# Graph attention in two layers: the attention's output turned by VectorE and by way of DRAM, scores and sums in column halves

## The chip, the cores and the metric

The kernel runs on one core of one Trainium2 chip. The metric is device time in microseconds for one execution. Before the change the median of three runs is 2571.63 us (2571.38 to 2572.58).

## What is computed

Two graph layers work on `x` of 16 graphs, 1024 nodes and 256 channels, all in float32. The first layer holds the attention that the change touches; the second (an aggregation over the graph, two matrix products with batch norms) runs beside it and after it. Cut to what matters:

```python
# --- layer 0 ---
h = jnp.maximum(_layernorm(x, axis=-1), 0.0)
...
g = jnp.einsum('bcn,bnm->bcm', fea, Wg)            # fea is h turned, Wg the weighted graph
g = jax.nn.relu(g * para.reshape(1, C, N))
q = jnp.transpose(g, (0, 2, 1)).reshape(B, N, h, hd).transpose(0, 2, 1, 3)
kv = (x @ kv_w).reshape(B, N, 2, h, hd).transpose(2, 0, 3, 1, 4)
k, v = (kv[0], kv[1])
attn = jax.nn.softmax(jnp.einsum('bhnd,bhmd->bhnm', q, k) * scale, axis=-1)
out = jnp.einsum('bhnm,bhmd->bhnd', attn, v)
return out.transpose(0, 2, 1, 3).reshape(B, N, C)
# x = x + that; then layer 1 on the result
```

There are four heads of 64 channels. The kernel takes the exponential without subtracting a maximum; a flag at the end would call a second, shifted version of the program if the sums had left a safe range.

## The kernel before

A *unit* is one graph `b`, one pair of heads `k` (128 channels) and one half `f` of the nodes that ask (512 of 1024): 64 units. A unit has four *steps*, each for 256 of the nodes that are asked about, so there are 256 steps, 16 to a graph.

`attention` (line 1032) writes the order out by hand, and the engines follow program order. In step `s` it issues:

1. `scores` (line 906): for two blocks of 128 asked nodes and the two heads, the products of keys and queries into PSUM (`sc`, two buffers[...]), then ScalarE's exponential into `p` (four buffers).
2. what is entered under `at_top` for this step: `sums` (line 977) and `finish` (line 1004) of the unit before.
3. what is entered under `adds`: `add_output` (line 1015) of the unit before.
4. VectorE's additions of the new `p` into `acc` (lines 941 and 944), from which the softmax's sums come.
5. `values` (line 946): the products of the step before's `p` with the values, into `o` (one PSUM buffer). After a unit's last step ScalarE copies `o` to `os` (line 964, two buffers).
6. work of the *background*, as much as a planner's costs say is due: queries, keys and values of the next graph, and layer 1's aggregation of the graph before. Its products go through the helper `product` (line 168), which splits each into two column halves: 128 contracted rows by 64 output rows, on each half of the array.
7. what is entered under `at_end`: `fold` (line 966), which turns and reduces `acc`.

If a unit's last values product falls in step `s`, its folds come at the end of steps `s` and `s+1`, `sums` in `s+3`, `finish` and `add_output` in `s+4`. The last unit of all has a shorter order. `finish` makes four TensorE transposes of 128x128 from `os` into PSUM (`ot`), and `add_output` multiplies them by the reciprocals of the sums (line 1018) and adds to `x` (line 1024).

The scores use the array in row halves: the two heads' 64 channels lie on partitions 0 to 63 and 64 to 127, and each product has 64 contracted rows and 128 output rows. The values and all background products use column halves. `sums` and `finish` use the whole array.

Loads run on SyncE's queue in program order (`adj`, `para`, `aht`, `ht`, `x`), stores of `y` (line 769), of `x` (line 785) and of `hsq_d` (line 412) on GpSimd's. `squares` and `gathered` (lines 402 and 414) already turn the layer's input by VectorE in squares of 32 and regroup it by way of DRAM.

Of the kernel before, what the change touches and what calls it, by code (L numbers as in the profile page):

```python
# [10 lines left out]
F32 = mybir.dt.float32  # L11
AF = mybir.ActivationFunctionType
ALU = mybir.AluOpType
AX = mybir.AxisListType
# [3 lines left out]
P = 128  # L18
# [5 lines left out]
def gnn_two_layers_kernel(  # L24
# [12 lines left out]
    nc = tc.nc  # L37
    B, N, C = x.shape
    H1 = w1_t.shape[1]
    NT = N // P  # L40
    CC = C // P
    HC = H1 // P
    HD = C // HEADS
    FB = 512
    NH = N // FB
    TH = 2
    NP = NT // TH
    HW = P // 2
# [3 lines left out]
    const = ctx.enter_context(tc.tile_pool(name="const", bufs=1))  # L52
# [17 lines left out]
    y1_d = [dram.tile([P, HC, FB], F32, name=f"y1_d{i}") for i in range(B * NH)]  # L70

    hsq_d = [dram.tile([P, CC, N], F32, name=f"hsq_d{b}") for b in range(B)]
    csum_d = [dram.tile([N], F32, name=f"csum_d{b}") for b in range(B)]
    dinv_d = dram.tile([N], F32, name="dinv_d")

    UNITS = B * CC * NH
# [3 lines left out]

    SQ = 32
    NS = P // SQ
    same = const.tile([P, NS, SQ], F32, name="same")
    nc.vector.tensor_reduce(
        same[:, 0, :], ident.rearrange("p (a r) -> p r a", r=SQ), AX.X, ALU.add
    )
    for i in range(1, NS):
        nc.vector.tensor_copy(same[:, i, :], same[:, 0, :])
    group = const.tile([P, NS], F32, name="group")
    nc.vector.tensor_reduce(group, ident.rearrange("p (a r) -> p a r", r=SQ), AX.X, ALU.add)  # L90

# [5 lines left out]
    def layers(shifted):  # L97
# [808 lines left out]
        def scores(b, k, f, g):  # L906


            made = []
            for m in (2 * g, 2 * g + 1):  # L910
                sc = ps_sc.tile([P, 2, FB], F32, tag="sc", name=f"sc_{b}_{k}_{f}_{m}")
                for e in range(2):
                    r = slice(e * HD, (e + 1) * HD)
                    nc.tensor.matmul(  # L914
                        sc[:, e, :],
                        ks[b][k][r, m * P : (m + 1) * P],
                        qs[b][k][r, f * FB : (f + 1) * FB],
                        start=True,
                        stop=True,
                    )  # L920
                pr = p4.tile([P, 2, FB], F32, tag="p", name=f"p_{b}_{k}_{f}_{m}")
                nc.scalar.activation(pr, sc, AF.Exp)  # L922
                made.append(pr)
            return made

        class Unit:
# [19 lines left out]
            def values(self, g, prs):  # L946

                b, k, f = self.at
                if g == 0:
                    self.o = ps_o.tile([P, FB], F32, tag="o", name=f"o_{self.name}")  # L950
                for i, pr in enumerate(prs):
                    m = 2 * g + i
                    for e in range(2):
                        r = slice(e * HD, (e + 1) * HD)
                        nc.tensor.matmul(  # L955
                            self.o[r, :],
                            vs[b][k][:, m, r],
                            pr[:, e, :],
                            start=(m == 0),
                            stop=(m == NT - 1),  # L960
                        )
                if g == NG - 1:
                    self.os = p2.tile([P, FB], F32, tag="os", name=f"os_{self.name}")
                    nc.scalar.copy(self.os, self.o)

            def fold(self, e):

# [9 lines left out]
            def sums(self):  # L977

                b, k, f = self.at
                J = FB // P  # L980
                if k == f == 0:
                    invs[b] = p2.tile([P, CC, NH, J, 2], F32, tag="inv", name=f"inv_{b}")
                self.inv = invs[b][:, k, f]
                pt = ps_t.tile([P, FB], F32, tag="t", name=f"sums_{self.name}")[:, : 2 * J * NS]
                nc.tensor.matmul(
                    pt,
                    same.rearrange("p a r -> p (a r)"),
                    self.part.rearrange("p e c -> p (e c)"),
                    start=True,
                    stop=True,  # L990
                )
                tmp = p1.tile([P, 2 * J, NS + 1], F32, tag="group", name=f"group_{self.name}")
                nc.vector.tensor_mul(
                    tmp[:, :, :NS],
                    pt.rearrange("p (c a) -> p c a", a=NS),
                    group.unsqueeze(1).to_broadcast([P, 2 * J, NS]),
                )
                nc.vector.tensor_reduce(tmp[:, :, NS], tmp[:, :, :NS], AX.X, ALU.add)
                nc.vector.reciprocal(
                    self.inv.rearrange("p j e -> p e j"),  # L1000
                    tmp[:, :, NS].rearrange("p (e j) -> p e j", e=2),
                )

            def finish(self):
# [9 lines left out]

            def add_output(self):
                b, k, f = self.at
                J, pt = FB // P, self.out
                nc.vector.tensor_mul(
                    self.os.rearrange("p (j e c) -> p j e c", j=J, e=2),
                    pt.rearrange("p (j e c) -> p j e c", j=J, e=2),  # L1020
                    self.inv.unsqueeze(3).to_broadcast([P, J, 2, HD]),
                )
                dst = xs[b][:, f * J : (f + 1) * J, k * P : (k + 1) * P]
                nc.vector.tensor_add(dst, self.os.rearrange("p (j c) -> p j c", c=P), dst)
                if k == CC - 1 and f == NH - 1:
                    inv = invs[b].rearrange("p k f j e -> p (k f j e)")
                    nc.vector.tensor_reduce(seen[:, 0, b : b + 1], inv, AX.X, ALU.max)
                    nc.vector.tensor_reduce(seen[:, 1, b : b + 1], inv, AX.X, ALU.min)
                if k == CC - 1:
                    complete.add((b, f))  # L1030

        def attention():

            units = [Unit(b, k, f) for b in range(B) for k in range(CC) for f in range(NH)]
            steps = [(u, g) for u in units for g in range(NG)]
            per_graph = CC * NH * NG
            before = None
            at_top, at_end, adds = {}, {}, {}
            bg, done, total, top = iter(()), 0.0, 0.0, False
            for s in range(len(steps) + 2):  # L1040
                if s < len(steps):
                    unit, g = steps[s]
                    b = unit.at[0]
                    if s % per_graph == 0:
                        run(bg)
                        top = False
                        bg, done = background(b), 0.0
                        total = (37.6 if b > 0 else 41.0) * (b + 1 < B) + 24.0 * (b > 0) + 4.0 * (b + 2 < B)
                        total += 13.7 * (0 < b < B - 2) + 27.4 * (b == B - 1) + 3.0 * (b == 0)

                        total -= 10.3 * (b == B - 1)
                    made = scores(*unit.at, g)
                    due = total * (s % per_graph + 1) / per_graph
                else:
                    due += 5.1
                for action in at_top.pop(s, ()):
                    action()
                if top:
                    done += advance(bg)
                    top = False  # L1060
                if s in adds:
                    adds.pop(s)()
                if s < len(steps):
                    for pr in made:
                        unit.add(pr)
                if before is not None:
                    (last, g_last), prs = before
                    last.values(g_last, prs)
                    if g_last == NG - 1:

                        one = (0, 0, 1, 1) if last.index == UNITS - 1 else (0, 1, 3, 4)
                        for e in range(2):
                            at_end.setdefault(s + one[e], []).append(lambda u=last, e=e: u.fold(e))
                        at_top.setdefault(s + one[2], []).append(last.sums)
                        at_top.setdefault(s + one[3], []).append(last.finish)
                        adds[s + one[3]] = last.add_output
                while done < due and not top:
                    cost = advance(bg)
                    if cost is None:
                        break  # L1080
                    if cost == TOP:
                        top = True
                        break
                    done += cost
                for action in at_end.pop(s, ()):
                    action()
                before = (steps[s], made) if s < len(steps) else None
            run(bg)
# [375 lines left out]
```

## Time and profile before

| What | Value |
|---|---|
| median of 3 runs | 2571.63 us |
| the profiled execution's own time | 2572.44 us |
| its span in the trace | 2570.6 us |
| mean granted TensorE clock | 0.989 |
| DMA engines busy (SyncE's queue, GpSimd's queue) | 33.7%, 9.5% |
| 1105 to 1250 us: TensorE, VectorE, ScalarE busy | 145.00, 109.83, 83.96 of 145.00 us |

The last row is a stretch of one graph in the middle of the attention. A matmul's start in the trace is recorded and its end is modelled, so costs on TensorE are read from one start to the next. A float32 product stands there as two records. In a shape such as 64\*128 the first number is the contracted rows and the second the output rows.

### The profile page before, as it was taken

The page shows a single profiled execution, that of the slowest core. Times are in us where ns is not written, and L with a number is a line of the kernel's source. Part 1 is how long each engine was busy: PE and PEld are TensorE (multiplying, and loading weights), DVE is VectorE, ACT ScalarE, POOL GpSimd, SP SyncE. Part 2 cuts the span into 40 slices and gives each one's busy share as a digit, 9 for nine tenths or more (in the row PEclk, how much of TensorE's full clock was granted, in tenths as well). Part 3 has the DMA queues.
Part 4 walks back from the last instruction along what each step waited for, and adds up shares of the span by engine and source line. Part 5 has one row for each costly group of instructions (what it writes and reads, how often), then busy time and mean ns, then how long its engine had stood idle before and what let it go on. Part 6 is the DMA issues. An engine that isn't in the chain of part 4 may idle for free. (4 is left out here: it accounts for less than half of the span.)

```text
span 2570.6 us, 31151 instructions
## 1 busy us (share of the span) xinstructions
PE 2497.0 (97%) x11403; PEld 913.0 (36%) x11403; DVE 1851.1 (72%) x2865; ACT 1432.0 (56%) x1978; POOL 396.8 (15%) x470
## 2 busy tenths in 40 slices
PE   8999999999999999999999999999999999999984
PEld 3333333333333333333333333333333333334443
DVE  4668786867777686878686777868686866656774
ACT  6765564647474746556464747464565634245553
POOL 1540100010101000010000010100101001036653
PEclk9999999999999999999999999999999999999997
DMA  4664425153434434351525344444425152255459
GB/s 140 211 223 146 157 85 198 58 205 99 173 128 155 148 148 135 110 181 61 209 70 185 119 158 142 156 136 151 139 95 194 45 187 96 103 217 213 174 199 364
DMA packets 149058, 392.81 MB, mean 153 GB/s; under 512 B 17304, under 2 KB 48544, under 8 KB 140960
## 3 DMA queue, kind: packets, MB, share of 16 engines
q1 hardware_dynamic: 126272, 297.39, 33.7%
q0 software_dynamic: 22624, 93.34, 9.5%
q8 instruction: 92, 1.51, 0.2%
q14 instruction: 70, 0.57, 0.1%
HBM read 301.47 MB, written 89.19 MB: 152 GB/s over the span
## 5 line engine op out<-in xcount | busy, mean ns | idle before, releaser
L922 ACT ACTIVATE p<-sc 128x1024 f32<-128x1024 f32 x512 | 495.1, 1020 | 495.5 <-PE sc L914 494.8
L944 DVE TENSOR_TENSOR acc<-acc,p 128x1024 f32<-128x1024 f32 x384 | 471.2, 1227 | 143.9 <-ACT p L922 123.2
L914 PE MATMUL sc<-q,k 64*128 64x512 f32 x2048 | 510.7, 617 | 6.5 <-ACT p L922 6.4
L955 PE MATMUL o<-p,v 128*64 128x512 f32 x2048 | 495.9, 605 | 0.0
L172 PE MATMUL pg<-w,h_a 128*64 128x512 f32 x1600 | 357.9, 592 | 3.0 <-DVE q L635 2.1
L172 PE MATMUL pa<-aht,h_b 128*64 128x512 f32 x1536 | 347.8, 595 | 3.5 <-ACT h_b L342 3.4
L914 PEld LDWEIGHTS sc<-q,k 64*128 64x128 f32 x2048 | 176.5, 186 | 328.9 <-issue 297.7
L481 ACT ACTIVATE w<-cbc,csum 128x512 f32<-128x512 f32 x256 | 285.5, 1167 | 0.0
L172 PE MATMUL py<-at,w 128*64 128x512 f32 x1024 | 230.7, 598 | 0.0
L468 DVE SCALAR_TENSOR_TENSOR w<-w,adj 128x1024 f32<-128x1024 f32 x128 | 157.4, 1230 | 87.5 <-ACT w L489 81.9
L955 PEld LDWEIGHTS o<-p,v 128*64 128x64 f32 x2048 | 124.1, 136 | 256.8 <-issue 243.3
L172 PEld LDWEIGHTS pg<-w,h_a 128*64 128x64 f32 x1600 | 114.6, 137 | 231.9 <-issue 213.4
L172 PEld LDWEIGHTS pa<-aht,h_b 128*64 128x64 f32 x1536 | 111.1, 137 | 217.5 <-issue 208.6
L769 POOL DMA_DIRECT2D y_d<-y x128 | 70.5, 551 | 701.9 <-ACT y L768 693.9
L768 ACT ACTIVATE y<-py,vec 128x512 f32<-128x512 f32 x128 | 87.5, 683 | 135.5 <-PE py L172 112.1
L94 POOL TENSOR_SCALAR lnsm_b<-mv_b 128x4 f32<-128x4 f32 x32 | 12.1, 379 | 834.5 <-DVE mv_b L320 834.4
L489 ACT ACTIVATE w<-w 128x1024 f32<-128x1024 f32 x128 | 135.2, 1056 | 1.7
L543 DVE TENSOR_TENSOR w<-w,w 128x1024 f32<-128x1024 f32 x112 | 132.7, 1215 | 1.5
L342 ACT ACTIVATE h_b<-x,lnsm_b 128x256 f32<-128x256 f32 x128 | 70.4, 608 | 110.4 <-DVE lnsm_b L331 110.4
L172 PEld LDWEIGHTS py<-at,w 128*64 128x64 f32 x1024 | 74.8, 138 | 147.2 <-issue 134.4
L172 PE MATMUL pk<-ht,kvw_f 128*64 128x512 f32 x512 | 117.9, 603 | 1.5 <-ACT ht L400 1.5
L172 PE MATMUL pv<-kvw_f,ht 128*64 128x256 f32 x1024 | 115.9, 379 | 0.0
(160 smaller groups left out, 2699.6 us busy)
## 6 DMA issues: line engine op xcount, KB each, us to landing
aht<-aht_d SPq DMA_DIRECT2D x224, 512.0 KB, 6.7
adj<-in_adj_dram SPq DMA_DIRECT2D x128, 512.0 KB, 5.6
y_d<-y POOLq DMA_DIRECT2D x128, 256.0 KB, 2.9
yin_f<-y_d SPq DMA_DIRECT2D x32, 1024.0 KB, 6.3
x<-in_x_dram SPq DMA_DIRECT2D x32, 512.0 KB, 5.2
para<-in_para_dram SPq DMA_DIRECT2D x64, 256.0 KB, 4.0
x_d<-x POOLq DMA_DIRECT2D x16, 1024.0 KB, 10.3
xo_f<-x_d SPq DMA_DIRECT2D x32, 512.0 KB, 8.8
```

What stands on the lines that cost most here:

```text
L172: nc.tensor.matmul(dst[r], left[:, r], right, start=start, stop=stop)
L342: nc.scalar.activation(self.h[:, t, :], self.src[:, t, :], AF.Relu, bias=self.sm[:, 1, t : t + 1], scale=self.sm[:, 0, t : t + 1], accum_o ...
L468: nc.vector.scalar_tensor_tensor(w, w, 1.0, a, op0=ALU.add, op1=ALU.mult)
L481: nc.scalar.activation(w[:, t, :].rearrange("p (t q) -> p t q", q=P), cbc[:, q * NT // NH : (q + 1) * NT // NH], AF.Abs, bias=csum[:, th * ...
L489: nc.scalar.activation(made[i], made[i], AF.Tanh, scale=-0.5 / C)
L543: nc.vector.tensor_sub(block(i)[part], block(x)[part], block(y)[part])
L768: nc.scalar.activation(y, made, AF.Identity, bias=b1[:, j : j + 1])
L769: nc.gpsimd.dma_start(out=y1_d[i][:, j, :], in_=y)
L914: nc.tensor.matmul(sc[:, e, :], ks[b][k][r, m * P : (m + 1) * P], qs[b][k][r, f * FB : (f + 1) * FB], start=True, stop=True,)
L922: nc.scalar.activation(pr, sc, AF.Exp)
L944: nc.vector.tensor_add(self.acc, self.acc, pr)
L955: nc.tensor.matmul(self.o[r, :], vs[b][k][:, m, r], pr[:, e, :], start=(m == 0), stop=(m == NT - 1),)
```

## The change

The output's turn leaves TensorE, save for the last unit. When a unit's `o` is complete, VectorE transposes it from PSUM into `os` in squares of 32x32, so that each group of 32 partitions still holds its own 32 channels, now with nodes along the partitions; GpSimd's queue stores `os` to a new DRAM tensor `out_d`, and in the next step four DMAs on SyncE's queue (`gather`) read it back into `os`, 32 partitions each, so that the 128 partitions are 128 nodes, in runs of 128 elements (512 B). `add_output` then multiplies `os` by the reciprocals in place, and adds it to `x`. Copying `o` by ScalarE and `finish` remain for the last unit only. The reciprocals are kept twice (`inv` gets an axis of two), since `os` now lies in four blocks of 32 channels, two for each head.

The scores are issued in column halves: four products of 64 contracted rows by 64 output rows for two heads, where there were two of 64 by 128. The matrix `same` of the sums is 64 columns wide in place of 128, and `sums` makes two products, one for each column half. `sums` moves from `at_top` to a new list `at_mid`, run after the background's part that may stand at the top and before `adds`; it stays in step `s+3`, after the scores and ahead of the values.

```diff
+    out_d = [dram.tile([P, FB], F32, name=f"out_d{u}") for u in range(B * CC * NH)]
...
-    same = const.tile([P, NS, SQ], F32, name="same")
+    same = const.tile([P, 2, SQ], F32, name="same")
...
                     r = slice(e * HD, (e + 1) * HD)
-                    nc.tensor.matmul(
-                        sc[:, e, :],
-                        ks[b][k][r, m * P : (m + 1) * P],
-                        qs[b][k][r, f * FB : (f + 1) * FB],
-                        start=True,
-                        stop=True,
-                    )
+                    for c in range(2):
+                        part = slice(c * HW, (c + 1) * HW)
+                        nc.tensor.matmul(
+                            sc[part, e, :],
+                            ks[b][k][r, m * P + c * HW : m * P + (c + 1) * HW],
+                            qs[b][k][r, f * FB : (f + 1) * FB],
+                            start=True,
+                            stop=True,
+                        )
...
-                    nc.scalar.copy(self.os, self.o)
+                    if self.index == UNITS - 1:
+                        nc.scalar.copy(self.os, self.o)
+                        return
...
+                    nc.vector.transpose(
+                        self.os.rearrange("p (j t s) -> p j t s", j=NS, s=SQ),
+                        self.o.rearrange("p (t j s) -> p j t s", j=NS, s=SQ),
+                    )
+                    nc.gpsimd.dma_start(out=out_d[self.index], in_=self.os)
+
+            def gather(self):
+
+                src = out_d[self.index].rearrange("(i s) (j r) -> j s i r", s=SQ, j=NS)
+                for j in range(NS):
+                    nc.sync.dma_start(
+                        out=self.os[j * SQ : (j + 1) * SQ].rearrange("s (i r) -> s i r", i=NS),
+                        in_=src[j],
+                    )
...
-                nc.tensor.matmul(
-                    pt,
-                    same.rearrange("p a r -> p (a r)"),
-                    self.part.rearrange("p e c -> p (e c)"),
-                    start=True,
-                    stop=True,
-                )
+                for e in range(2):
+                    nc.tensor.matmul(
+                        pt[e * HW : (e + 1) * HW],
+                        same.rearrange("p a r -> p (a r)"),
+                        self.part.rearrange("p e c -> p (e c)"),
+                        start=True,
+                        stop=True,
+                    )
...
+                    blocks = self.os.rearrange("p (m s) -> p m s", s=SQ)
+                    nc.vector.tensor_mul(
+                        blocks,
+                        blocks,
+                        self.inv.rearrange("p e x j -> p (e x j)")
+                        .unsqueeze(2)
+                        .to_broadcast([P, NS * J, SQ]),
+                    )
+                    dst = dst.rearrange("p j (i s) -> p j i s", s=SQ)
+                    nc.vector.tensor_add(
+                        dst, self.os.rearrange("p (i j s) -> p j i s", i=NS, j=J), dst
+                    )
...
+                for action in at_mid.pop(s, ()):
+                    action()
                 if s in adds:
                     adds.pop(s)()
...
-                        at_top.setdefault(s + one[2], []).append(last.sums)
-                        at_top.setdefault(s + one[3], []).append(last.finish)
+                        (at_top if last.index == UNITS - 1 else at_mid).setdefault(
+                            s + one[2], []
+                        ).append(last.sums)
+                        if last.index == UNITS - 1:
+                            at_top.setdefault(s + one[3], []).append(last.finish)
+                        else:
+                            at_top.setdefault(s + 1, []).append(last.gather)
                         adds[s + one[3]] = last.add_output
```

More of the change, by code (lines that the diff above doesn't have):

```diff
@@ L82, in gnn_two_layers_kernel @@
     NS = P // SQ
-    same = const.tile([P, NS, SQ], F32, name="same")
-    nc.vector.tensor_reduce(
-        same[:, 0, :], ident.rearrange("p (a r) -> p r a", r=SQ), AX.X, ALU.add
-    )
-    for i in range(1, NS):
-        nc.vector.tensor_copy(same[:, i, :], same[:, 0, :])
+    same = const.tile([P, 2, SQ], F32, name="same")
+    for i in range(2):
+        nc.vector.tensor_reduce(
+            same[:, i, :], ident.rearrange("p (a r) -> p r a", r=SQ), AX.X, ALU.add
+        )
     group = const.tile([P, NS], F32, name="group")
@@ L981, in sums @@
                 if k == f == 0:
-                    invs[b] = p2.tile([P, CC, NH, J, 2], F32, tag="inv", name=f"inv_{b}")
+                    invs[b] = p2.tile([P, CC, NH, 2, 2, J], F32, tag="inv", name=f"inv_{b}")
                 self.inv = invs[b][:, k, f]
                 pt = ps_t.tile([P, FB], F32, tag="t", name=f"sums_{self.name}")[:, : 2 * J * NS]
-                nc.tensor.matmul(
-                    pt,
-                    same.rearrange("p a r -> p (a r)"),
-                    self.part.rearrange("p e c -> p (e c)"),
-                    start=True,
-                    stop=True,
-                )
+                for e in range(2):
[6 more added lines that the diff above has]
+                    )
                 tmp = p1.tile([P, 2 * J, NS + 1], F32, tag="group", name=f"group_{self.name}")
@@ L999, in sums @@
                 nc.vector.reciprocal(
-                    self.inv.rearrange("p j e -> p e j"),
-                    tmp[:, :, NS].rearrange("p (e j) -> p e j", e=2),
+                    self.inv,
+                    tmp[:, :, NS]
+                    .rearrange("p (e j) -> p e j", e=2)
+                    .unsqueeze(2)
+                    .to_broadcast([P, 2, 2, J]),
                 )
@@ L1016, in add_output @@
                 b, k, f = self.at
[L1017 to L1022, printed above, removed]
-                dst = xs[b][:, f * J : (f + 1) * J, k * P : (k + 1) * P]
-                nc.vector.tensor_add(dst, self.os.rearrange("p (j c) -> p j c", c=P), dst)
+                J = FB // P
+                dst = xs[b][:, f * J : (f + 1) * J, k * P : (k + 1) * P]
+                if self.index == UNITS - 1:
+                    nc.vector.tensor_mul(
+                        self.os.rearrange("p (j e c) -> p j e c", j=J, e=2),
+                        self.out.rearrange("p (j e c) -> p j e c", j=J, e=2),
+                        self.inv[:, :, 0, :]
+                        .rearrange("p e j -> p j e")
+                        .unsqueeze(3)
+                        .to_broadcast([P, J, 2, HD]),
+                    )
+                    nc.vector.tensor_add(dst, self.os.rearrange("p (j c) -> p j c", c=P), dst)
+                else:
+                    blocks = self.os.rearrange("p (m s) -> p m s", s=SQ)
+                    nc.vector.tensor_mul(
+                        blocks,
+                        blocks,
+                        self.inv.rearrange("p e x j -> p (e x j)")
+                        .unsqueeze(2)
+                        .to_broadcast([P, NS * J, SQ]),
+                    )
+                    dst = dst.rearrange("p j (i s) -> p j i s", s=SQ)
+                    nc.vector.tensor_add(
+                        dst, self.os.rearrange("p (i j s) -> p j i s", i=NS, j=J), dst
+                    )
                 if k == CC - 1 and f == NH - 1:
-                    inv = invs[b].rearrange("p k f j e -> p (k f j e)")
+                    inv = invs[b].rearrange("p k f e x j -> p (k f e x j)")
                     nc.vector.tensor_reduce(seen[:, 0, b : b + 1], inv, AX.X, ALU.max)
@@ L1037, in attention @@
             before = None
-            at_top, at_end, adds = {}, {}, {}
+            at_top, at_mid, at_end, adds = {}, {}, {}, {}
             bg, done, total, top = iter(()), 0.0, 0.0, False
@@ L1073, in attention @@
                             at_end.setdefault(s + one[e], []).append(lambda u=last, e=e: u.fold(e))
-                        at_top.setdefault(s + one[2], []).append(last.sums)
-                        at_top.setdefault(s + one[3], []).append(last.finish)
+                        (at_top if last.index == UNITS - 1 else at_mid).setdefault(
[3 more added lines that the diff above has]
+                            at_top.setdefault(s + one[3], []).append(last.finish)
+                        else:
+                            at_top.setdefault(s + 1, []).append(last.gather)
                         adds[s + one[3]] = last.add_output
```

## The prediction

> **What bounds the kernel now.** I read the page's busy shares first, then what TensorE waits for, then the groups of TensorE rows by shape, and last the order of time around one step. Times are microseconds; the mean of a group is in ns.
>
> ```profile
> PE 2497.0 (97%) x11403; PEld 913.0 (36%) x11403; DVE 1851.1 (72%) x2865; ACT 1432.0 (56%) x1978; POOL 396.8 (15%) x470
> ```
>
> TensorE is busy for 97% of the span. Its longest list of waits (one line for each thing waited for: total, times, longest) is short, and the lines after this one are smaller still:
>
> ```profile
> PE htp L397 <- ACT h_a L342: 8.5, 1, 8.5
> PE pt_f L1390 <- ACT y_f L1382: 6.9, 6, 5.2
> PE sc L914 <- ACT p L922: 6.4, 3, 5.2
> PE sums L985 <- DVE part L973: 5.0, 1, 5.0
> ```
>
> So through the attention, to about 2246, time is what TensorE's own stream takes. The rows that the change touches, by shape (busy, mean | idle before):
>
> ```profile
> L914 PE MATMUL sc<-q,k 64*128 64x512 f32 x2048 | 510.7, 617 | 6.5 <-ACT p L922 6.4
> L955 PE MATMUL o<-p,v 128*64 128x512 f32 x2048 | 495.9, 605 | 0.0
> L1010 PE MATMUL ot<-ident,os 128*128 128x128 f32 x256 | 42.5, 289 | 0.3 <-DVE group L993 0.3
> L985 PE MATMUL sums<-part,same 128*128 128x32 f32 x128 | 26.3, 288 | 5.0 <-DVE part L973 5.0
> L964 ACT COPY os<-o 128x512 f32<-128x512 f32 x64 | 37.5, 585 | 82.4 <-PE o L955 82.4
> L972 DVE STREAM_TRANSPOSE acc<-acc 128x512 f32<-128x512 f32 x128 | 89.0, 695 | 0.0
> L1018 DVE TENSOR_TENSOR os<-ot,inv 128x512 f32<-128x512 f32 x64 | 44.0, 688 | 80.8 <-PE ot L1010 80.8
> ```
>
> Each float32 product is two records. What a stretch really costs is read from starts, since ends are modelled; two steps in order of time (start, length, x records):
>
> ```profile
> 1219.59 1.99 PE L914 MATMUL sc<-q,k 64*128 64x512 f32 x8
> 1221.51 0.41 PE L985 MATMUL sums<-part,same 128*128 128x32 f32 x2
> 1221.84 1.94 PE L955 MATMUL o<-p,v 128*64 128x512 f32 x8
> 1223.61 1.90 PE L172 MATMUL pv<-kvw_f,ht 128*64 128x256 f32 x16
> 1225.34 3.60 PE L172 MATMUL pa<-aht,h_b 128*64 128x512 f32 x16
> 1228.87 1.99 PE L914 MATMUL sc<-q,k 64*128 64x512 f32 x8
> 1230.79 0.66 PE L1010 MATMUL ot<-ident,os 128*128 128x128 f32 x4
> 1231.38 1.94 PE L955 MATMUL o<-p,v 128*64 128x512 f32 x8
> ```
>
> Two records run side by side, one on each half of the array, and a pair starts every 429 ns inside one shape: eight records are 4 x 0.429 = 1.72. The `sc` stretch takes 1.92 and `o` 1.77 to the next start. From the starts of all records: going from a product in column halves (128*64) to `sc` (64*128, two row halves) takes 522 instead of 429 (+93), the next pair inside `sc` 533 (+104, its 128-column weights not loaded ahead), `sc` to `o` 519 (+90), the next pair inside `o` 480 (+51). Together 338 ns in each of 256 steps, 86.5 us: the price of changing the shape twice.
>
> **What the Trainium skill says.** "TensorEngine Tiling (Array Packing)", Key Properties: changing the tiling mode drains TensorE, while tiles of one mode run independently. The trace agrees: +90 to +93 at every change of shape, none between `o` and a product. The same page's Tiling Modes list 64x64 with four tiles as a mode beside 128x64. "TensorE: Matmul & The Clock Gate", LDWEIGHTS: load time goes with columns, not rows; here 187 against 137 ns, and the exposed part 104 against 51. "PSUM — Partial Sum Buffer", on bank collisions: column tiles may write one bank together, row tiles may not; the heads already write two banks (`sc[:, e, :]`), and nothing in this trace shows four tiles at once.
>
> **The change, part by part.** The profiled execution took 2572.44 (span 2570.6); the median of the runs shown is 2571.63. I work against 2572.4.
>
> *Output turn off TensorE.* `finish` goes for 63 of 64 units. At 1230.79 the turn delays `o` to 1231.38. Over all units: three gaps of 130 plus 203 to `o`, 592 ns; the 520 ahead of it stays as the 519 from `sc` to `o`. 63 x 0.592 = **-37.3**, all on the path.
>
> *What replaces it.* ScalarE loses 63 copies of 585 (37 us, not on the path). VectorE gains 63 block transposes from PSUM: the SBUF row of this size is 695, and "Perfetto Trace Analysis", Optimizing Scalar/DVE Operations, puts a PSUM access some 65 ns above an SBUF one, so an estimated 0.76, 48 us in all. VectorE goes to about 75% (1851 + 48 of 2519), and loses 80.8 of waiting for `ot`. The transpose stands behind the new unit's first `acc` addition (L941), and `o` has one buffer, so the next unit's first values product waits for it. In all 63 places that addition ends 0.7 to 2.9 after the old copy began, and that product starts 0.5 (one place), 2.0 and mostly 3.3 to 5.5 after the transpose would end. Cost on the path 0; if the cover went, the overrun itself.
>
> *Way through DRAM.* One store on POOL per unit (like `y_d`, 0.54 to issue, 2.9 to land) and four gathers on SP (like `ht<-hsq_d`, 0.43 to issue, 4.0 to land). A gather waits for the store, and later loads wait behind it. Ready is about transpose end + 0.6 + 2.9, near the start of the step where the gather is issued. I placed the 63 fours in SP's queue by program order with these prices: 16 loads of `aht` move, by 3.2 at most, and still land 4.2 or more before their products; `adj`, `para` and `ht` loads don't move, as SP is waiting for buffers then. POOL's next entries come later than the transpose in any case. `add_output`, three steps (26 us) after the gather, finds its data some 20 us old; if it didn't, the `acc` additions behind it on VectorE would wait, and then the exponentials. Transfers: 32,256 more packets of 512 B, between 24 and 110 ns each (the SP queue's mean of 110 for 2.36 KB, whole or by bytes), 2 to 9% more of engines 43% busy. Cost 0; the unknown is a few us in the first graph, where POOL is busiest.
>
> *Sums in column halves.* Same place before `o`. Now 132 + 206 + the 51 inside `o`, 389 ns; afterwards the shape is that of `o`, so the leave costs no drain, but two short weight loads (137 each, 54 apart) and the next one remain, about 0.28. Bounds: saving 0.05 to 0.25; I take 0.1 x 63 = **-6**.
>
> *Scores in column halves.* Sixteen records a step of 64*64 instead of eight. If four tiles run at once, still four groups at 429. The question is the change of shape. Upper bound of gain: all 338 ns gone, -86.5. Upper bound of loss: the four tiles don't start together (below). The tiling page has 64x64 as another mode, so I keep both drains and shorten only the load: 533 becomes 480, less 12 for two more staggered starts of 6 ns. 0.041 x 256 = **-10**.
>
> Sum: 2572.4 - 37.3 - 6 - 10 = **2519**.
>
> **The rivals.**
>
> *A, forecast: drains stay, loads are shorter.* 2519; its own range 2505 to 2540. For: every change of shape in the trace costs the same 90 to 93, whichever two shapes. Chance 0.52.
>
> *B: no drain between 64*64 and 128*64.* The hardware might count the column split alone as the mode. Then 86.5 goes, and sums cost about 0.2 less: 2572.4 - 37.3 - 12 - 86.5 = 2437; half of it 2480. Against: row halves differ, as they do today. Chance 0.24.
>
> *C: the gain is partly eaten.* Twice the instructions in `sc`, or a load or `o` released late. TensorE needs a weight load and a product each 107 ns; the trace shows 108 sustained (`pv`) and nothing faster. At 50 to 160 ns a step: 2540 to 2570. Chance 0.12.
>
> *D, slower: tiles start in two stages.* The program lists each tile's two records together; today two tiles nonetheless start 6 ns apart. If the look-ahead reaches only two tiles, the second row half begins one record late, and every `sc` stretch is 429 longer before it can hand over: +110, less 43: 2639. It decides from about 170 ns a step (43 / 256). Against: the same reordering works for two tiles now. Chance 0.12.
>
> That the turn isn't really taken off TensorE can't be; the diff leaves it for the last unit alone.
>
> **How the numbers follow.** A kernel like this shows a difference from about 0.2%, 5 us. A and B are 0.76; part of C, to 2550, makes 0.8. So 2440 to 2550. Faster is A, B and nearly all of C, 0.86; within 0.2% the end of C, 0.02; slower D, 0.12.
>
> **What would show it.** `ot` down to 4 records and the step with the turn 0.59 shorter proves the first term. Starts inside `sc`: groups of four about 429 apart, first gap near 480, hand-overs near 520 (A) or 429 (B), pairs half a record late (D). VectorE waiting for DMA at the multiplication of `os`, or TensorE at `o` for the transpose, would make the zeros wrong; the forecast fails above all if a change of shape to 64*64 costs something else than the 90 seen now.

## The result, and the profile after

The changed kernel takes 2550.93 us (median of 4 runs, 2546.20 to 2553.29) against 2571.51 of the kernel before in the same comparison: ratio 0.9917, 95% interval 0.9900 to 0.9934. It is faster by some 21 us, and not by the 53 that were forecast; the time lies 0.9 us above the stated range, 2440 to 2550.

The page after, with the rows that answer to those shown of before. The first line is busy time (share of the span) x instructions; in the rows the columns are busy, mean in ns, and idle time before with what ended it:

```profile
PE 2444.5 (96%) x13327; PEld 828.8 (33%) x13327; DVE 1888.9 (74%) x2926; ACT 1397.1 (55%) x1915; POOL 434.5 (17%) x533
```

```profile
L916 PE MATMUL sc<-q,k 64*64 64x512 f32 x4096 | 500.5, 604 | 7.3 <-ACT p L924 7.3
L957 PE MATMUL o<-p,v 128*64 128x512 f32 x2048 | 495.0, 604 | 0.3 <-DVE os L971 0.3
L971 DVE STREAM_TRANSPOSE os<-o 128x512 f32<-128x512 f32 x63 | 44.6, 708 | 0.0
L1055 DVE TENSOR_TENSOR os<-os,inv 128x512 f32<-128x512 f32 x63 | 42.9, 681 | 0.3 <-DMA cbc<-csum_d 0.3
L1006 PE MATMUL sums<-part,same 128*64 128x32 f32 x256 | 19.9, 234 | 5.0 <-DVE part L993 5.0
```

The turn is off TensorE. VectorE hardly waits for the way through DRAM (L1055: 0.3 us), and TensorE hardly waits for VectorE's transposes (L957: 0.3 us). TensorE is still the busiest, but three of the longest lines in its list of waits are new (total, times, longest):

```profile
PE pk L172 <- DMA ht<-hsq_d: 12.8, 2, 12.0
PE pv L172 <- DVE q L577: 9.8, 13, 0.8
PE pv L172 <- ACT v L672: 6.2, 13, 0.5
```

One is mainly a single big wait; the other two come 13 times each, once in each of 13 graphs.

**Step against step.** There are 256 steps, and each begins with the first record of `sc`. Taking the length of each step from one such start to the next, in both traces, gives the change of every step. Nearly all of these are a sum of a few numbers:

| Steps | Change of one | Sum |
|---|---|---|
| each of the 256 (scores) | -0.04 | -10.2 |
| the 63 with `sums`, besides | -0.22 | -13.9 |
| the 63 that held `finish`, besides | -0.59 | -37.2 |
| the seventh of the second to fourteenth graph, besides | +1.67 | +21.7 |
| the first of the second graph, besides | +16.8 | +16.8 |
| four steps in the first and the last two graphs, besides | | +2.5 |

That is 61.3 won on TensorE and 41.0 given back: 20.3, and the spans differ by 20.9. TensorE's mean granted clock was 0.989 before and 0.986 after; since nearly all steps differ by these few numbers, the clock doesn't explain them, save part of the second graph's loss (below). So the question is the two losses.

**The loss in the seventh step.** The ninth graph serves as the example; it begins at 1155.50 before and at 1155.02 after. First TensorE in order of time, before (start, length, records; in brackets the wait just ahead and what ended it):

```profile
1210.62 1.99 PE L914 MATMUL sc<-q,k 64*128 64x512 f32 x8
1212.54 1.94 PE L955 MATMUL o<-p,v 128*64 128x512 f32 x8
1214.31 5.35 PE L172 MATMUL pv<-kvw_f,ht 128*64 128x256 f32 x48
1219.59 1.99 PE L914 MATMUL sc<-q,k 64*128 64x512 f32 x8
```

and after:

```profile
1208.51 1.95 PE L916 MATMUL sc<-q,k 64*64 64x512 f32 x16
1210.38 1.94 PE L957 MATMUL o<-p,v 128*64 128x512 f32 x8
1212.15 1.90 PE L172 MATMUL pv<-kvw_f,ht 128*64 128x256 f32 x16
1214.81 1.95 PE L172 MATMUL pv<-kvw_f,ht 128*64 128x256 f32 x16 [0.76 <-DVE q L577]
1217.23 1.95 PE L172 MATMUL pv<-kvw_f,ht 128*64 128x256 f32 x16 [0.47 <-ACT v L672]
1219.11 1.95 PE L916 MATMUL sc<-q,k 64*64 64x512 f32 x16
```

TensorE comes to this step 2.11 earlier and leaves it 0.48 earlier, which is what it had at the graph's start. The products `pv` are three groups of 16 records here, and they take their PSUM buffers (the kernel calls them banks) from two in turn. The second group's buffer still holds the last product of the next graph's queries, until VectorE has added it (L577). The third group's buffer is that of the first group, until ScalarE has made its two copies of it (L672). VectorE before, then after:

```profile
1213.33 1.26 DVE L529 TENSOR_TENSOR q<-q,para 128x512 f32<-128x512 f32 x2
1214.51 0.68 DVE L577 TENSOR_TENSOR q<-pg,q 128x512 f32<-128x512 f32 x1
```

```profile
1212.89 1.26 DVE L529 TENSOR_TENSOR q<-q,para 128x512 f32<-128x512 f32 x2
1214.07 0.68 DVE L577 TENSOR_TENSOR q<-pg,q 128x512 f32<-128x512 f32 x1
```

ScalarE before, then after:

```profile
1214.02 1.23 ACT L531 ACTIVATE q<-q 128x512 f32<-128x512 f32 x2 [0.36 <-DVE q L529]
1215.16 1.92 ACT L922 ACTIVATE p<-sc 128x1024 f32<-128x1024 f32 x2
1216.96 0.65 ACT L672 COPY v<-pv 128x256 f32<-128x256 f32 x2
```

```profile
1213.59 1.23 ACT L531 ACTIVATE q<-q 128x512 f32<-128x512 f32 x2 [0.36 <-DVE q L529]
1214.72 1.92 ACT L924 ACTIVATE p<-sc 128x1024 f32<-128x1024 f32 x2
1216.53 0.65 ACT L672 COPY v<-pv 128x256 f32<-128x256 f32 x2
```

The wait that ends last is the one for ScalarE. In all 13 graphs the third group of `pv` starts 0.05 after the end of the second copy; in the kernel before it starts 0.14 to 0.16 after it. So before, TensorE arrived within 0.1 of the moment when this buffer came free, and no wait stood in the profile. The buffer of L577 had then been free for 0.8; the new wait for it comes earlier in the step and is covered by the other.

ScalarE goes without a gap from L531 to the copies, and L531 waits for VectorE's L529, which stands just ahead of L577. So VectorE sets the time for both buffers. L577 starts 59.01 and 59.05 after its graph's start, at the end of a stretch in which VectorE has no gap over 0.15 us, 33.7 us long before and 34.4 after. The stretch starts with two additions into `acc` (L944, after the change L946) that had waited 2.3 for ScalarE's exponentials, at 1180.80 and 1179.65. That is 25.30 and 24.63 after the graph's start. What TensorE saves in the first three steps lets VectorE start its stretch 0.67 earlier; what it saves in the next three doesn't reach VectorE, which is busy throughout.

**The loss at the second graph.** GpSimd's order of time after, in the first graph:

```profile
173.38 0.58 POOL L287 DMA_DIRECT2D aht_d<-one  x1
173.96 0.56 POOL L975 DMA_DIRECT2D out_d<-os  x1
```

and SyncE's queue:

```profile
145.66 0.33 SPq L446 DMA_DIRECT2D cbc<-csum_d  x1
177.44 3.44 SPq L981 DMA_DIRECT2D os<-out_d  x4
180.98 1.43 SPq L184 DMA_DIRECT2D adj<-in_adj_dram  x3
182.51 6.55 SPq L420 DMA_DIRECT2D ht<-hsq_d  x8
```

VectorE had the third unit's transpose done at 153.27. Its store was issued 20.7 later, since GpSimd was still at the differences of adjacency blocks that the first graph's background puts on it (lines 259 to 287). The gather on SyncE's queue waits for that store from 146 to 177, and the loads of `adj` and `ht` stand behind it. Before, the same three `adj` loads were issued from 141.45 on. VectorE then waits 17.7 for `adj`, and TensorE for `ht`:

```profile
191.25 1.97 PE L172 MATMUL pk<-ht,kvw_f 128*64 128x512 f32 x4 [12.04 <-DMA ht<-hsq_d]
```

In the kernel before, the same step has no such wait:

```profile
180.91 5.32 PE L172 MATMUL pk<-ht,kvw_f 128*64 128x512 f32 x24
```

A second wait for `ht` adds 0.74. That is 12.8 of the 16.8. Most of the rest is TensorE itself: the 24 records of `pk` in this step take 5.25 from their first start to the next step before, and 9.28 after, of which 0.74 is the second wait. The granted clock was 0.50 from 185 to 195 us and 0.84 from 195 to 205, where it was 1.00 in the kernel before.

### The profile page after: what moved, and what is told of

It is laid out like the page before. It is cut to its first block, busy times and chain, and to the rows that moved or that the text cites. A ratio compares the mean times of both kernels' runs of the same rounds, so it can differ in the third digit from the quotient of the medians.

```text
span 2549.7 us, 35551 instructions
## 1 busy us (share of the span) xinstructions
PE 2444.5 (96%) x13327; PEld 828.8 (33%) x13327; DVE 1888.9 (74%) x2926; ACT 1397.1 (55%) x1915; POOL 434.5 (17%) x533
## 3 DMA queue, kind: packets, MB, share of 16 engines
q1 hardware_dynamic: 162560, 313.92, 37.2%
## 5 line engine op out<-in xcount | busy, mean ns | idle before, releaser
L946 DVE TENSOR_TENSOR acc<-acc,p 128x1024 f32<-128x1024 f32 x384 | 471.2, 1227 | 139.1 <-ACT p L924 118.1
L916 PE MATMUL sc<-q,k 64*64 64x512 f32 x4096 | 500.5, 604 | 7.3 <-ACT p L924 7.3
L957 PE MATMUL o<-p,v 128*64 128x512 f32 x2048 | 495.0, 604 | 0.3 <-DVE os L971 0.3
L975 POOL DMA_DIRECT2D out_d<-os x63 | 35.6, 565 | 1260.3 <-DVE os L971 1260.3
L916 PEld LDWEIGHTS sc<-q,k 64*64 64x64 f32 x4096 | 131.4, 132 | 350.5 <-issue 316.4
L957 PEld LDWEIGHTS o<-p,v 128*64 128x64 f32 x2048 | 124.7, 136 | 303.0 <-issue 283.9
L342 ACT ACTIVATE h_b<-x,lnsm_b 128x256 f32<-128x256 f32 x128 | 70.4, 609 | 133.2 <-DVE lnsm_b L331 133.2
L172 PE MATMUL pv<-kvw_f,ht 128*64 128x256 f32 x1024 | 121.7, 382 | 16.0 <-DVE q L577 9.8
L172 PE MATMUL pk<-ht,kvw_f 128*64 128x512 f32 x512 | 120.8, 614 | 14.3 <-DMA ht<-hsq_d 12.8
```

Source lines behind the costliest of these rows:

```text
L172: nc.tensor.matmul(dst[r], left[:, r], right, start=start, stop=stop)
L342: nc.scalar.activation(self.h[:, t, :], self.src[:, t, :], AF.Relu, bias=self.sm[:, 1, t : t + 1], scale=self.sm[:, 0, t : t + 1], accum_o ...
L916: nc.tensor.matmul(sc[part, e, :], ks[b][k][r, m * P + c * HW : m * P + (c + 1) * HW], qs[b][k][r, f * FB : (f + 1) * FB], start=True, sto ...
L946: nc.vector.tensor_add(self.acc, self.acc, pr)
L957: nc.tensor.matmul(self.o[r, :], vs[b][k][:, m, r], pr[:, e, :], start=(m == 0), stop=(m == NT - 1),)
```

## The experiments

Each run was compared with the kernel before on the same chip. What they did to the seventh step is seen best inside one graph: the last two columns give when the seventh and the eighth step start, in us from the start of the ninth graph (from the starts in the traces).

| Kernel | Median us | Ratio to before (95%) | Seventh step starts | Eighth step starts |
|---|---|---|---|---|
| before | 2571.5 | | 55.12 | 64.09 |
| the change | 2550.9 | 0.9917 (0.9900 to 0.9934) | 53.49 | 64.09 |
| halves_only | 2552.2 | 0.9925 (0.9909 to 0.9942) | 54.66 | 64.06 |
| rows_again | 2558.6 | 0.9948 (0.9931 to 0.9964) | 53.73 | 64.14 |
| copy_scalar | 2541.2 | 0.9883 (0.9866 to 0.9899) | 53.49 | 63.47 |
| fold_later | 2530.4 | 0.9838 (0.9821 to 0.9854) | 53.49 | 62.75 |
| store_sp | 2539.1 | 0.9869 (0.9852 to 0.9885) | 53.49 | 64.08 |
| fold_store | 2521.3 | 0.9805 (0.9789 to 0.9821) | 53.49 | 62.75 |
| first_graph_old | 2535.5 | 0.9857 (0.9840 to 0.9873) | 53.49 | 64.07 |
| best | 2530.9 | 0.9838 (0.9821 to 0.9854) | 53.49 | 63.62 |
| fold_first | 2519.1 | 0.9795 (0.9781 to 0.9808) | 53.49 | 62.74 |

**halves_only: the change without the turn.** Copy, `finish` and the old output for all units:

```diff
-                    if self.index == UNITS - 1:
+                    if True:
                         nc.scalar.copy(self.os, self.o)
                         return
...
-                        if last.index == UNITS - 1:
-                            at_top.setdefault(s + one[3], []).append(last.finish)
-                        else:
-                            at_top.setdefault(s + 1, []).append(last.gather)
+                        at_top.setdefault(s + one[3], []).append(last.finish)
```

> The change without the turn: scores and sums in column halves, the output turned by TensorE and copied by ScalarE as before, for all units. Both theories: scores -0.04 in each of 256 steps (-10.2 us) and sums -0.22 in 63 steps (-13.9 us), and no 16 us at the start of the second graph. Theory (TensorE meets VectorE's backlog in the seventh step of a graph, whatever made TensorE earlier): up to 0.46 us a graph, gained in the six steps before, is given back there, so 2547 to 2554. Rival (the loss in the seventh step comes from the 63 transposes on VectorE or from the traffic): nothing is given back, 2547 to 2548, and the wait of pv for q stays out of the trace.

Measured 2552.2. The seventh step gives back 0.48, all that the six before had won. The wait for `q` that the theory named stays out of the trace, as the rival had it: the buffer of L577 was free some 0.25 before it was needed. What is there is the wait for ScalarE's copies, and the third group starts 0.05 after them:

```profile
PE pv L172 <- ACT v L672: 3.4, 13, 0.3
```

Two things follow. The loss in the seventh step doesn't need the transposes on VectorE: the eighth step starts at 64.06 here too. And the turn by VectorE, as the change has it, brought about nothing (2552.2 without, 2550.9 with it): nearly all of the 37 us won on TensorE went into the two losses.

**copy_scalar: the transposes on VectorE left out.**

```diff
-                    nc.vector.transpose(
-                        self.os.rearrange("p (j t s) -> p j t s", j=NS, s=SQ),
-                        self.o.rearrange("p (t j s) -> p j t s", j=NS, s=SQ),
-                    )
+                    nc.scalar.copy(self.os, self.o)
```

> The change with ScalarE's copy of o to os in place of VectorE's 63 transposes in squares; store, gathers and the rest stay. It leaves out the turn inside the squares, so its output is another. Theory (the seventh step starts when VectorE is through its unbroken stretch, and the transpose of the graph's second such unit lies in that stretch with 0.7): the step gives back about 0.95 in place of 1.63 in 13 graphs, 2540 to 2544, and 16 us are still lost at the second graph. Rival (the transposes are paid by the waits for ot that went): 1.63 as before, 2549 to 2553.

Measured 2541.2, and the seventh step gives back 1.07 in place of 1.67. So one transpose of 0.7 lies in VectorE's unbroken stretch and counts there with 0.6. That the eighth step starts at 64.09 in the change as in the kernel before is a coincidence of two near-equal numbers: VectorE enters its stretch 0.67 earlier, and spends it on the transpose. Between halves_only and this run VectorE's stretch is as long (33.8 in both), and TensorE has the turn in the one and not in the other: the eighth step starts 0.59 earlier here. That is the price of the one turn ahead of the stretch.

**fold_later: 1.4 us less on VectorE ahead of L577.**

```diff
-                        one = (0, 0, 1, 1) if last.index == UNITS - 1 else (0, 1, 3, 4)
+                        one = (0, 0, 1, 1) if last.index == UNITS - 1 else (1, 1, 3, 4)
```

> The change with one number moved: a unit's first fold (a transpose and a reduction on VectorE, 1.4 us) stands at the end of the step after, beside the second fold. Theory (VectorE's backlog ahead of the additions of the queries' last products holds the two banks that pv needs): the backlog is 1.4 us shorter there, the seventh step of a graph loses at most 0.3 us in place of 1.63, the wait of pv for q is gone, 2526 to 2536 us. Rival (traffic or TensorE's clock): as after the change, 2546 to 2553.

Measured 2530.4. The eighth step starts 1.34 earlier, and VectorE's stretch is as much shorter (33.1). The wait of `pv` for L577 is gone: that buffer is now free 0.4 before it is needed. The 0.34 that the step still gives back is the wait for ScalarE's copies, which again end 0.05 ahead of the third group; it is too short for the list of waits, which leaves out gaps of up to 0.15. With halves_only and copy_scalar this shows that VectorE's stretch, through ScalarE, sets the start of the eighth step: what is taken from VectorE inside the stretch moves it, and what is taken from TensorE moves it only ahead of the stretch. Of the 20.5 us between this run and the change, 3.6 are not of this kind: the second graph's first step loses 13.2 here in place of 16.8.

**store_sp: the first graph's stores away from GpSimd.**

```diff
-                    nc.gpsimd.dma_start(out=out_d[self.index], in_=self.os)
+                    if self.at[0] > 0:
+                        nc.gpsimd.dma_start(out=out_d[self.index], in_=self.os)
...
             def gather(self):
 
+                if self.at[0] == 0:
+                    nc.sync.dma_start(out=out_d[self.index], in_=self.os)
```

> The change with the store of out_d of the first graph's four units issued by SyncE's queue just ahead of the gathers, in place of GpSimd's. Theory (in the first graph the third store stands 20 us behind the graph's combinations on GpSimd, and adj and ht behind its gather): the second graph's first step loses nothing in place of 16.1 us, 2533 to 2538. Rival (the added traffic in the first graph delays adj and ht): 2546 to 2553.

Measured 2539.1, one above the expected. The second graph's first step loses 2.0 in place of 16.8, so the queue on GpSimd was the cause and not the traffic. But its fourth step now loses 5.1: there TensorE waits 3.2 for VectorE (L553), which had itself waited 3.9 for an `adj` load on SyncE's queue. The queue's trouble was moved, not ended.

**first_graph_old: the first graph turned by TensorE.** The condition for the old path gains one term, in the three places where it stands:

```diff
-                    if self.index == UNITS - 1:
+                    if self.at[0] == 0 or self.index == UNITS - 1:
```

> The change with the first graph's four units turned by TensorE as before, and the other 59 by VectorE and DRAM. Theory (the 16 us come from GpSimd's queue in the first graph alone): they are gone, four turns of 0.59 come back, 2535 to 2540. It tells also what SyncE's stores cost in the run before: that one kept a loss of 5 us in the second graph's fourth step, which must be gone here. Rival (the traffic of the second graph does it): over 2545.

Measured 2535.5. The first step of the second graph is 16.0 shorter than in the change, and the fourth step has no loss. The four turns cost their 0.59 each.

**fold_store: both losses at once.**

> Both edits: the first fold one step later and the first graph's stores on SyncE's queue. If the two losses are separate and are all that was lost: 2551 - 21 - 16 = 2514, within 2509 to 2521. If one hides the other, over 2525.

Measured 2521.3, between the two cases and at the edge of the first: the sum of the two runs alone would be 2518.6. That sum counts some of the second graph's loss twice, since fold_later alone had 3.6 of it. The seventh step still gives back 0.34 a graph, and the second graph's fourth step still loses 4.8.

**best: a third edit.** The two edits of fold_later and first_graph_old, and

```diff
-                yield from weave(queries(b + 1), (0, double(w)), (9, islice(norm, 5)))
+                yield from weave(queries(b + 1), (0, double(w)), (10, islice(norm, 5)))
```

> The change with three edits: the first fold one step later, the first graph's four units turned by TensorE, and the statistics of the second norm one background piece later (1.0 us less on VectorE ahead of the last queries). If VectorE's stretch was the only thing ahead of the seventh step, the 0.34 that the later fold left is gone too: 2512 to 2518. If the norm's own consumers come late instead, 2519 to 2530.

A miss: 2530.9, just above the second range. With the statistics later, the eighth step starts at 63.62, 0.87 later than by the fold alone. The list of TensorE's waits shows who is late now:

```profile
PE pv L172 <- ACT v L672: 12.1, 13, 1.0
```

ScalarE's work for the norm (L342, two of them in 1.08) now stands between the exponentials and the copies of `v`; in fold_later it stands ahead of L531. L577 starts 0.10 earlier than in fold_later, and the copies end 0.87 later, as much as the eighth step is late. So the unplanned test shows that the step waits for the copies, and not for L577.

**fold_first: best without that edit.**

> The change with two edits: the first fold one step later and the first graph's four units turned by TensorE; the norm stays where it was. If the two losses are separate: 2535.5 less 13 times 1.3 to 1.4, 2516 to 2519, and the wait of pv for the copies of v, which the later norm had brought, falls to what it was or less. If the fold's gain needs the stores on SyncE: over 2525.

Measured 2519.1 (5 runs, 2517.05 to 2520.66), the fastest of all: ratio 0.9795, 0.9781 to 0.9808 to the kernel before. It falls on the case in which the two losses are separate, and no wait of `pv` is in its list. That this is also the 2519 of the forecast is chance: the forecast had neither these edits nor the losses that are left, and took too little for the sums.

**rows_again: the scores in row halves again.**

```diff
-                    for c in range(2):
-                        part = slice(c * HW, (c + 1) * HW)
-                        nc.tensor.matmul(
-                            sc[part, e, :],
-                            ks[b][k][r, m * P + c * HW : m * P + (c + 1) * HW],
...
+                    nc.tensor.matmul(
+                        sc[:, e, :],
+                        ks[b][k][r, m * P : (m + 1) * P],
...
```

> The change with the scores in row halves as before (two products of 64 by 128). Theory: 0.04 more in each of 256 steps, of which the seventh step of 13 graphs takes back some 0.24, since VectorE sets its start: 2557 to 2560. Rival (column halves bring nothing, the noise of the clock does): 2549 to 2553. If they bring more through a hand-over without a drain: over 2562.

Measured 2558.6. Column halves are worth some 8 us in the whole. The intervals of this run and of the change just overlap, so the trace decides: it has the 0.04 back in each step, and the seventh gives back 1.46 in place of 1.67.

## Why the prediction was wrong

**Right: the output's turn off TensorE.** 0.592 was worked out for each turn, and 0.59 went in each of 63 steps.

**Right: the scores in column halves.** Four records of `sc` start 6 to 7 ns apart, the next four 480 after the first (429 between later ones), and the hand-overs stay at 523 and 519. That is case A, 0.04 a step; no drain went (B), and no tile starts half a record late (D). The Trainium skill's page "TensorEngine Tiling (Array Packing)", Key Properties, says that a change of mode drains TensorE, and that held for 64x64 as well: changing to it or from it costs 523 and 519 ns, where a next group in the same mode costs 429.

**Mis-sized: the sums.** 0.1 was taken, 0.22 measured. The four records of `sums` start at 0, 7, 79 and 86 ns, and `o` 52 after the last: 0.14 in place of 0.34. The prediction had laid two weight loads one after the other and the next one behind them, 0.28 with the 0.05 inside `o`; the starts leave no room for that.

**Wrong: "Cost on the path 0" for what replaces the turn.** The prediction tested VectorE's transposes against one consumer, the next unit's first values product, and that part held: TensorE waited 0.3 us for `o`. It didn't ask which other buffers TensorE gets back from VectorE, or from ScalarE when that waits for VectorE, nor whether these keep up with a TensorE that is 1.64 us earlier. VectorE was counted at 75% on the mean, and has no gap in the 34 us ahead of L577. The term that was missing is 13 x 1.67 = 21.7. Only 13 x 0.6 = 8 of it is the transposes' own price (copy_scalar). The rest is a credit that was never there: the sum took every ns won on TensorE as won in the end, and halves_only shows that even 0.46 a graph wasn't.

**Wrong: "Cost 0" for the way through DRAM.** The prediction placed the gathers in SyncE's queue, but gave every store the same time after its transpose, and wrote that GpSimd's next entries come later and that `adj` and `ht` loads don't move. It named the first graph as the unknown and put it at a few us. What counts is the entries *ahead* of the store in program order: in the first graph they held it for 20.7 us, and the wait was passed on to a queue of loads. 16.8 us.

Neither of the two signs named for wrong zeros appeared: VectorE waiting at the multiplication of `os`, and TensorE waiting at `o`, stayed at 0.3 us each. The costs came out elsewhere.

Case C, "the gain is partly eaten", is what happened, at a chance of 0.12, and its 2540 to 2570 holds the time. Of the causes that it named, "a load ... released late" is what the second graph shows; that its range holds the time is luck, since it was made from 50 to 160 ns in every step, and not from a loss once a graph.

## What to carry to other kernels

When an engine is busy for 97%, ask before crediting a saving on it who gives back its buffers in each stretch, and whether that engine has idle time there: where a step's start doesn't move with the busy engine's work, it belongs to another. A wait of zero in the profile may be two engines that arrive together. When two waits stand in one step, follow the one that ends last: here it was ScalarE's, behind VectorE's. Of a transfer that goes through two queues, look at what stands ahead of it in the first one, in the busiest stretch of that queue, and at what stands behind it in the second.

## What the runs showed of the hardware

VectorE's 32x32 transpose of 128x512 takes 708 ns out of PSUM and 695 in SBUF (L972 before), in means: 13 more, where an estimate from the Trainium skill's "Perfetto Trace Analysis", Optimizing Scalar/DVE Operations, had put 65. Four float32 products of 64x64 run at once on TensorE in the 429 ns that two of 64x128 took. A store of 256 KB and a gather of 64 KB landed after 2.4 and 2.1 us (medians), less than the rows taken for them (2.9 and 4.0). A store on GpSimd's queue stood 20.7 us behind that engine's other entries, and the loads behind its gather on SyncE's queue were held with it.
